# Two-layer image-prompt attention: even entries laid image first with one mixed value group, halves of the output added by VectorE out of PSUM, low parts of two splits on GpSimd

## The chip, the cores and the metric

One core of a Trainium2 chip runs the whole program in one launch. The metric is device time in microseconds (us), lower is better. Engines are named as the profile names them: PE multiplies matrices (PEld loads its weights), DVE is VectorE, ACT is ScalarE, POOL is GpSimd, SP issues most transfers.

## The reference

Two attention layers follow one another over 16 batch entries of 256 queries and 256 context rows (E = 512 wide), with 320 channels (C) in 20 heads (H) of 16 (D). The first layer, cut to what matters:

```python
q = heads(x @ Wq)
text, image = ctx[:, :77], ctx[:, 77:]              # 77 and 179 rows
a_text  = softmax(q @ heads(text @ Wk).T * scale)
a_image = softmax(q @ heads(image @ Wk_ip).T * scale + semantic_term)
out = a_text @ heads(text @ Wv) + mask * (a_image @ heads(image @ Wv_ip))
x = x + out.reshape(...) @ Wout + bout
```

The semantic term is built from a second, narrow softmax over the products of the text rows with the image rows (in the kernel `tokens0`, `semantic0`, `rs`). The second layer does the same kind of work with 252 text rows and 4 image rows; the change hardly touches it.

## The kernel before

The code's comments call the layers 0 and 1. A layer is cut into 80 slots: slot k treats entry `b = k // 5` and one group of four heads, `g = k % 5`. A layer-0 slot does, per half t of the context:

- `score0`: scores with queries on the partitions, S, from which DVE takes two maxima per head, of text and image (L747, L748); `maxima0` (L754) turns them for the stacked operands.
- `turned0`: transposed scores T, keys on the partitions (L770); ACT writes their exponentials into a P tile (L773), and POOL multiplies these by the semantic weights `rs` (L776).
- `attend0(k-1)`: 24 matmuls (L805) with values `vr` into the values' bank, also called P in the profile. `vr` holds three blocks of 128 context rows per entry: rows 0 to 127 as text (its mask zeroes the image rows), rows 0 to 127 as image, rows 128 to 255 as image. Text and image outputs lie in the two halves of the bank.
- `settle0`: DVE transposes the bank (L816), takes reciprocals of the sums (L819, L820) and multiplies (L822) into `tmp`; POOL adds the halves (L823) into `hsn`, and copies the last group (L825).

Around the slots run tasks with written due times in slots. For each pair c of entries `keys0(c)` loads the context of both, splits it into a high and a low part (tiles `cta`, `ctb`; high on ACT, low on POOL, L169) and makes the keys of both (128x156 text, 128x360 image). `tokens0` makes the text-image products, `values0_` the values: three groups per entry, each of 12 matmuls of 320 columns (`wC` holds the text weights and `wD` the image weights). `queries0` splits the input `xq` into `hq` (L284 on ACT, L285 on POOL, L286 on DVE). After an entry's last slot `gather` transposes `hsn` on DVE (L835), and `finish` splits the result into `ho` (L284 on ACT, L285 and L286 on DVE) and projects it (L611, L614). PE's order and the start (`begin`, all engines) are written by hand; inside a slot the other engines' instructions are ordered by a scheduler.

Of the kernel before, what the change touches and what calls it, by code (L numbers as in the profile page):

```python
# [35 lines left out]
CH = H * D  # L36

# [15 lines left out]
def xattn2(  # L53
# [60 lines left out]
    words, slots = {"ctb": 1024, "cta": 1024, "raw": 512, "rawc": 512, "both": 2 * (S - T0), "kb": 936, "si": 256, "sp": 128, "wC": 2 * 4 * (H * D + NIP), "mt": S, "mx": 2, "tmp": (NG + 1) * 48, "kst": 4 * S, "rs": 2 * S, "P": 4 * S}, {}  # L114
# [47 lines left out]
    def halves(hi, lo, src, eng=nc.vector, loaded=False):  # L162
        order = queued if loaded else lambda inst: inst
        if len(hi.shape) != len(src.shape):
            src = src.rearrange("p (d h) -> p d h", d=D)[:, :, :H]
        order(nc.scalar.copy(hi, src))
        for i, (to, *at) in enumerate(lo if isinstance(lo, list) else [(lo,)]):
            at = (slice(None), *at)
            order((nc.gpsimd if i and loaded else eng).tensor_sub(to, src[at], f(hi)[at]))  # L169
# [22 lines left out]
    def in_turn(parts, wait, tag="raw", eng=nc.vector, later=False):  # L192

        ahead, parts, tags = [], list(parts), tag.split()
        for i in range(len(parts) + 1):
# [4 lines left out]
            if i:  # L200
                halves(*ahead.pop(0), eng, wait)
# [52 lines left out]
    def evacuate(hi, lo, out, m):  # L254

        if m < 2:
            return halves(hi, lo, out)
        hi, lo = hi[:64], lo[:64]
        both = buf("both", list(hi.shape), bufs=2)
        nc.scalar.copy(hi, out[:64])  # L260
        nc.scalar.copy(both, out[64:])
        nc.vector.tensor_sub(out[:64], out[:64], f(hi))
        nc.vector.tensor_add(lo, out[:64], both)

    def context(b, n, wait=0):

        tiles, parts = [], []
        for k in range(0, 4, 3 - n):
            src = cT_d[:, b * S : (b + n) * S].rearrange("(k p) t -> p k t", p=128)[:, k : k + 3 - n]
            ct = buf("cta" if n == 1 or k < 2 else "ctb", [128, 2, 512], FR, bufs=SIZES["CTA" if n == 1 or k < 2 else "CTB"], name="ct")  # L270
            split = lambda t: t.rearrange("p (k t) -> p k t", t=n * S)
            parts.append((src, split(ct[:, 0]), split(ct[:, 1])))
            tiles.append(ct)
        yield from in_turn(parts, wait, "rawc raw" if b == 2 and n == 2 else "rawc", nc.gpsimd if wait and b != 2 else nc.vector, n == 2 and b > 2)
        if n == 2:
            return lambda s, k: tiles[k][:, s].rearrange("p (b t) -> p b t", b=2)
# [3 lines left out]
    def split(src, neg, eng, tag, place=None):  # L280
# [5 lines left out]
        order(nc.vector.scalar_tensor_tensor(hl[:, 2], f(hl[:, 2]), neg, src[:, 2], op0=ALU.mult, op1=ALU.add))  # L286
        return hl

    ct = [buf(t, [128, 2, 512], FR, bufs=2, name="ct") for t in ("cta", "cta", "ctb", "ctb")]
    ct0 = {0: lambda s, k, tiles=ct: tiles[k][:, s].rearrange("p (b t) -> p b t", b=2)}  # L290
# [10 lines left out]
    for k in range(4):  # L301
        first["c", k] = cT_d[k * 128 : (k + 1) * 128, : 2 * S], ct[k][:, 0], ct[k][:, 1], ("rawc", "raw")[k // 2]
# [8 lines left out]
    ks = [const_tile([128, 4, S], f"ks{i}", FR) for i in range(SIZES["NR"])]  # L311
# [54 lines left out]

    def keys0(c):
        if c not in ct0:
# [3 lines left out]
            get("m0t", 2 * c - 1)  # L372
            ct0[c] = yield from tiles
        ct = ct0[c]
        kt = kts[c] = buf("kb", [128, 3, 2, 2, T0 + 1], FR, name="kt")
        for m in range(3):
            kst = buf("kst", [128, 2, 2, S], FR, bufs=SIZES["KST"])
            for w, lo, hi, a, z in ((wk0, 0, T0 + 1, 0, T0), (wki0, T0 - 1, S, T0, S)):
                kp = bank()[:, : 2 * (hi - lo)].rearrange("p (b t) -> p b t", b=2)
                prod_m(kp, w, m, lambda s, k: ct(s, k)[:, :, lo:hi], 4)  # L380
                n = 64 if m == 2 else 128
                evacuate(kst[:, 0, :, a:z], kst[:, 1, :, a:z], kp[:, :, a - lo : z - lo], m)
                if a:
                    keys_out(kd[0][c], m, kst)
                else:
                    nc.gpsimd.tensor_copy(kt[:n, m, :, :, :T0], f(kst[:n, :, :, :T0]))
                yield

    def keys_first():

        ct = ct0[0]
        kst = [buf("kst", [128, 2, 2, S], FR, bufs=SIZES["KST"]) for i in range(2)]
        kst.append(buf("ho", [128, 5 * S], FR)[:, : 4 * S].rearrange("p (s b t) -> p s b t", s=2, b=2))
# [3 lines left out]
        kp = [out(0, T0 + 1) for m in range(3)]  # L397
        for k in range(4):
            for m in range(3):
                terms = ((0, 0), (0, 1), (1, 0))[: 3 if m < 2 else 2]  # L400
                for i, (a, c) in enumerate(terms):
                    mm(kp[m], wk0(a, k, m), ct(c, k)[:, :, : T0 + 1], start=k + i == 0, stop=k == 3 and i == len(terms) - 1)
            yield
        for m in range(3):
            n = 64 if m == 2 else 128
            evacuate(kst[m][:, 0, :, :T0], kst[m][:, 1, :, :T0], kp[m][:, :, :T0], m)
            nc.gpsimd.tensor_copy(kt[:n, m, :, :, :T0], f(kst[m][:n, :, :, :T0]))
        yield
        for m in range(3):
            kp = out(T0 - 1, S)  # L410
            prod_m(kp, wki0, m, lambda s, k: ct(s, k)[:, :, T0 - 1 : S], 4)
            evacuate(kst[m][:, 0, :, T0:], kst[m][:, 1, :, T0:], kp[:, :, 1:], m)
            keys_out(kd[0][0], m, kst[m], slice(0, 1))
            yield
        for m in range(3):
            keys_out(kd[0][0], m, kst[m], slice(1, 2))
        yield

    def values0_(b):
        ct, i = ct0[b // 2], b % 2  # L420
        V = vr[(b + 2) % 3]
        for t, (w,), lo, sc in ((0, wv0, 0, tmask[:, 0:1]), (1, wvi0, 0, tmask[:, 1:2]), (2, wvi0, 128, 1.0)):
            vp = bank()[:, :320]
            prod(vp, lambda s, k: ct(s, k)[:, i, lo : lo + 128], lambda s, k: w(s, k), 4)
# [3 lines left out]
            yield  # L428
        return V

    def tokens0(b):

        ct, i = ct0[b // 2], b % 2
        stack = buf("M", [TR, 2, S], FR, bufs=SIZES["M"])
        M = stack[:T0]
        nc.gpsimd.memset(f(M[:, :, :T0]), 0.0)
        gp = bank()
        lo = 64
        prod(gp[:T0, : S - lo], lambda s, k: ct(s, k)[:, i, :T0], lambda s, k: ct(s, k)[:, i, lo:S], 4)
        src = gp[:T0, T0 - lo : S - lo]  # L440
# [213 lines left out]
    def semantic0(b):  # L654
# [41 lines left out]
        for t in range(2):  # L696
            mm(rp[:, t], mh[:T0, 0, t * 128 : (t + 1) * 128], tph[:, 1], start=True, stop=False)
            mm(rp[:, t], mh[:T0, 1, t * 128 : (t + 1) * 128], tph[:, 0], start=False, stop=True)
# [7 lines left out]
    def stacks0(k, parts="KQTM"):  # L706
        b, g = divmod(k, NG)
        Q, K = QK[k] = qs[k % SIZES["NR"]], ks[k % SIZES["NR"]]
        for part in parts:
# [4 lines left out]
            elif g < SIZES["NR"]:  # L714
# [3 lines left out]
                else:  # L718
                    dma(K[XROW : XROW + TR, :, T0:], mh[:, 0:1, T0:].to_broadcast([TR, 4, S - T0]))
# [19 lines left out]
    def score0(k, t):  # L739
# [7 lines left out]
        nc.vector.tensor_reduce(mn[:, t, :, 0], sp[:, :, :T0], axis=AX.X, op=ALU.max)  # L747
# [721 lines left out]
```

## Time and profile before

| what | us |
|---|---|
| median of 3 runs (range) | 1493.27 (1488.1 to 1494.71) |
| profiled execution: time, span | 1491.16, 1489.3 |
| busy: PE, DVE, ACT, POOL | 1426.1, 1172.7, 886.0, 1212.5 |
| layer 0, ten slots (one pair of entries) in the steady part | 74.5 |

The chain of waits is 75% PE, 8% DVE, 5% DMA and 5% POOL. Layer 0 ends near 700 us of the span. Rows of instructions give start, duration, engine, line, operation and tile; a row of the stretches gives, after its length, each engine's busy time and count, then the clock granted to PE, the share of the DMA engines and GB/s. Neighbouring instructions of one engine overlap in the records, so a group of matmuls is timed best from its first start to the next group's.

### The profile page before, as it was taken

The numbers are of one execution on the slowest core, as the hardware profiler recorded it, in microseconds if no ns is written. First come the engines' busy times: TensorE is split into PE (matmuls) and PEld (weight loads), VectorE is DVE, ScalarE is ACT, GpSimd is POOL, SyncE is SP. The second block draws the span as 40 slices with busy tenths as digits, with TensorE's granted clock in tenths as the row PEclk, the third lists the DMA queues.
The fourth block names the chain that finished last, engine by engine and source line by source line (L and its number), as shares of the span: only waits on it lengthen the run. The fifth ranks groups of instructions, "written<-read, shape, count | busy, mean of one in ns | idle before, by whom it ended". The sixth has DMA issues, their size and how long they took to land.

```text
span 1489.3 us, 36118 instructions
## 1 busy us (share of the span) xinstructions
PE 1426.1 (96%) x12740; PEld 1155.8 (78%) x12740; DVE 1172.7 (79%) x2595; ACT 886.0 (59%) x1975; POOL 1212.5 (81%) x1302
## 2 busy tenths in 40 slices
PE   8799999999999899789999999999999999999998
PEld 7678888888888788577777777777777777777766
DVE  5467777777777787778887788788878887888787
ACT  5346565656565555456665666566666665666563
POOL 4359797979797877798698779878987898788887
PEclk9799999999999999799999999999999999999999
DMA  7867777778787776684534444444444444444411
GB/s 237 212 178 222 205 223 205 222 204 224 200 228 202 208 204 176 165 222 151 155 104 126 123 117 119 133 122 116 121 133 119 121 121 124 125 122 102 112 32 55
DMA packets 230986, 234.32 MB, mean 157 GB/s; under 512 B 39127, under 2 KB 200678, under 8 KB 230790
## 3 DMA queue, kind: packets, MB, share of 16 engines
q1 hardware_dynamic: 228598, 230.71, 55.8%
q8 instruction: 102, 1.67, 0.5%
q10 hardware_dynamic: 2208, 1.30, 0.4%
q14 instruction: 78, 0.64, 0.1%
HBM read 118.04 MB, written 77.04 MB: 131 GB/s over the span
## 4 chain that ended last, share of the span: by engine, by line
PE 75%; DVE 8%; DMA 5%; POOL 5%; issue 3%; ACT 3%; SPq 1%; ACTq 0%; DVEq 0%; POOLq 0%
PE X L944 15%; PE X L241 14%; PE P L805 6%; PE X L611 5%; PE S L746 5%; PE P L956 5%; PE P L966 4%; PE T L770 4%; PE T L895 3%; PE S L901 3%; PE X L614 2%; PE X L251 2%; PE X L580 2%; DVE mn L748 2%; POOL P L776 1%
## 5 line engine op out<-in xcount | busy, mean ns | idle before, releaser
L776 POOL TENSOR_TENSOR P<-P,rs 128x512 f32<-128x512 f32 x320 | 414.4, 1318 | 86.6 <-ACT P L773 79.8
L935 POOL TENSOR_TENSOR wt<-P,ctb 128x512 f32<-128x512 f32 x318 | 408.4, 1308 | 74.1 <-ACT ctb L933 74.0
L944 PE MATMUL X<-ctb,gm 128*128 128x512 f32 x1120 | 306.3, 402 | 5.8 <-DVE wt L945 5.7
L773 ACT ACTIVATE P<-T 128x512 f32<-128x512 f32 x320 | 175.4, 594 | 159.4 <-PE T L770 112.4
L945 DVE TENSOR_TENSOR wt<-X,wt 128x512 f32<-128x512 f32 x320 | 216.1, 681 | 42.2 <-PE X L944 37.3
L944 PEld LDWEIGHTS X<-ctb,gm 128*128 128x128 f32 x1120 | 195.0, 188 | 39.3 <-DVE wt L945 8.7
L915 ACT ACTIVATE P<-T 128x512 f32<-128x512 f32 x320 | 173.1, 593 | 75.1 <-PE T L895 72.1
L933 ACT ACTIVATE ctb<-P 128x512 fp32r<-128x512 f32 x320 | 186.6, 627 | 38.0 <-PE X L944 35.2
L903 DVE TENSOR_REDUCE mn<-S 128x4 fp32r<-128x1008 f32 x160 | 191.5, 1197 | 0.0
L748 DVE TENSOR_REDUCE mn<-S 128x4 fp32r<-128x716 f32 x160 | 142.4, 890 | 0.0
L805 PE MATMUL P<-P,vr 128*32 128x256 f32 x1920 | 125.9, 393 | 6.1 <-DVE tmp L822 2.2
L746 PE MATMUL S<-ks,qs 125*128 125x256 f32 x640 | 117.4, 307 | 6.2 <-DMA ks<-M 4.1
L746 PEld LDWEIGHTS S<-ks,qs 125*128 125x128 f32 x640 | 89.0, 195 | 40.8 <-issue 22.1
L1035 POOL TENSOR_TENSOR r<-u,rs 128x40 f32<-128x40 f32 (+2 forms) x17 | 108.7, 6395 | 3.1 <-DVE u L1032 3.0
L770 PE MATMUL T<-qs,ks 127*128 127x256 f32 x640 | 107.7, 291 | 0.4 <-DMA qs<-mt 0.3
L747 DVE TENSOR_REDUCE mn<-S 128x4 fp32r<-128x308 f32 x160 | 74.5, 466 | 31.1 <-PE S L746 31.0
L816 DVE STREAM_TRANSPOSE nt<-P 128x512 f32<-128x512 f32 x80 | 57.1, 713 | 52.9 <-PE P L805 52.2
L805 PEld LDWEIGHTS P<-P,vr 128*32 128x32 f32 x1920 | 56.7, 112 | 47.4 <-POOL P L776 7.3
L770 PEld LDWEIGHTS T<-qs,ks 127*128 127x128 f32 x640 | 91.6, 197 | 1.7 <-DMA qs<-mt 0.8
L956 PE MATMUL P<-P,v1t 128*32 128x256 f32 x1280 | 85.7, 385 | 0.0
L966 PE MATMUL P<-wt,zone 128*32 128x256 f32 x1280 | 84.4, 379 | 0.0
L241 PE MATMUL X<-wC,cta 128*128 128x324 f32 (+1 forms) x474 | 78.4, 312 | 0.0
(305 smaller groups left out, 2976.8 us busy)
## 6 DMA issues: line engine op xcount, KB each, us to landing
qd<-q SPq DMA_DIRECT2D x96, 256.0 KB
qs<-tph SPq DMA_DIRECT2D x64, 320.0 KB
rawc<-in_cT_dram SPq DMA_DIRECT2D x60, 256.0 KB
qs<-qd SPq DMA_DIRECT2D x80, 192.0 KB
ks<-kd SPq DMA_DIRECT2D x80, 192.0 KB
ks<-kd SPq DMA_DIRECT2D x160, 96.0 KB
qs<-qd SPq DMA_DIRECT2D x160, 96.0 KB
kd<-kst SPq DMA_DIRECT2D x57, 256.0 KB
```

What stands on the lines that cost most here:

```text
L241: last = mm(out, lhs(a, k), rhs(b, k), start=i == 0, stop=i == len(terms) - 1)
L746: mm(sp[:, h], Q[: XROW + T0, h, t * 128 : (t + 1) * 128], K[: XROW + T0, h], start=True, stop=True)
L770: mm(st[p][:, j], K[:KS0, 2 * p + j, t * 128 : (t + 1) * 128], Q[:KS0, 2 * p + j], start=True, stop=True)
L773: exp = anchor(nc.scalar.activation(pt, st[p], AF.Exp, scale=SCALE))
L776: anchor(nc.gpsimd.tensor_mul(pt, pt, rs[:, t : t + 1].to_broadcast([128, 2, S])))
L805: mm(pv[32 * s : 32 * s + 32, o : o + S], v[:, vt, h : h + 32], P[k, s // 2][:, t, s % 2], start=vt < 2, stop=vt != 1,)
L903: anchor(nc.vector.tensor_reduce(maxes[k + 2][:, t], sp[:, :, :T1], axis=AX.X, op=ALU.max))
L915: anchor(nc.scalar.activation(P[k, u][:, t], st[u], AF.Exp, scale=SCALE))
L933: nc.scalar.activation(R[k, u][:, t], P[k, u][:, t], AF.Copy, scale=0.5)
L935: anchor(eng.tensor_sub(W[k, u][:, t], P[k, u][:, t], f(R[k, u][:, t])))
L944: mm(yp, gm[:, gb], R[k, u][:, kt], start=i == 0, stop=i == len(blocks[n]) - 1)
L945: nc.vector.tensor_mul(W[k, u][:, n], yp, W[k, u][:, n])
```

## The change

Even entries are laid with their 179 image rows first and the 77 text rows behind, odd entries text first as before. One group of 12 matmuls, `values_mixed`, then makes the image values that lie beside text in both entries of a pair (51 rows of the even one, 51 of the odd one), so a pair has five value groups instead of six. The context tiles become padded tiles of 1129 words with 51 words of zeros ahead and sides of 539 words; their splits are written in two pieces, text and image, and so are the image keys' evacuations. The masks in the sum column of `vr` now differ by entry and are set by `mark(b)` for each entry, in place of one `marks()`; the memsets of `M` in `tokens0` go to the start. `settle0` multiplies into the values' bank instead of `tmp`, and a DVE reduction over a stride of 128 words adds the halves into `hsn`. `split_pool` makes the low parts of layer 0's `ho` on POOL; `queries0` makes the last low part of `hq` on POOL too. In layer 1 the copy of the last group goes into DVE's multiplication.

PE, ahead of slot 10c+5: 24 value matmuls stood behind the transposed scores of the slot before (`ident_r` rows are L754, the next slot's maxima).

```order
350 L746 MATMUL S<-ks_99,qs_95 128x256 x4
351 L770 MATMUL T<-qs_97,ks_101 128x256 x4
352 L241 MATMUL X<-wD,cta_81 128x320 x3
353 L241 MATMUL X<-wD,cta_82 128x320 x3
354 L241 MATMUL X<-wD,ctb_83 128x320 x3
355 L241 MATMUL X<-wD,ctb_84 128x320 x3
356 L241 MATMUL X<-wD,cta_81 128x320 x3
357 L241 MATMUL X<-wD,cta_82 128x320 x3
358 L241 MATMUL X<-wD,ctb_83 128x320 x3
359 L241 MATMUL X<-wD,ctb_84 128x320 x3
360 L754 MATMUL X<-ident_r,mn_566 8x128 x2
```

The same place after:

```order
342 L840 MATMUL S<-ks_99,qs_95 128x256 x4
343 L865 MATMUL T<-qs_97,ks_101 128x256 x4
344 L252 MATMUL X<-wD,cta_81 128x320 x3
345 L252 MATMUL X<-wD,cta_82 128x320 x3
346 L252 MATMUL X<-wD,ctb_83 128x320 x3
347 L252 MATMUL X<-wD,ctb_84 128x320 x3
348 L849 MATMUL X<-ident_r,mn_614 8x128 x2
```

One group of 12 is gone there; elsewhere in the steady part PE's order is the same, with 180 columns for 192 and 154 for 156 in some groups.

POOL, in slots 10c+5 and 10c+6 of a pair, before (P rows are L776; `rawc` is the loaded context):

```order
205 L776 TENSOR_TENSOR P_120<-P_120,rs_115 128x512
206 L776 TENSOR_TENSOR P_121<-P_121,rs_115 128x512
207 L169 TENSOR_TENSOR cta_81<-rawc_118,cta_81 128x512
208 L823 TENSOR_TENSOR hsn<-tmp_808 128x8x16
209 L169 TENSOR_TENSOR cta_82<-rawc_117,cta_82 128x512
210 L776 TENSOR_TENSOR P_122<-P_122,rs_115 128x512
211 L776 TENSOR_TENSOR P_123<-P_123,rs_115 128x512
```

And after:

```order
226 L327 TENSOR_TENSOR hq_270<-xq_91,hq_270 128x512
227 L329 TENSOR_TENSOR hq_270<-xq_91,hq_270 64x256
228 L871 TENSOR_TENSOR P_121<-P_121,rs_116 128x512
229 L871 TENSOR_TENSOR P_122<-P_122,rs_116 128x512
230 L934 TENSOR_TENSOR ho_195<-hT_1335,ho_195 128x256
231 L871 TENSOR_TENSOR P_121<-P_121,rs_116 128x512
232 L871 TENSOR_TENSOR P_122<-P_122,rs_116 128x512
233 L175 TENSOR_TENSOR cta_81<-rawc_119,cta_81 128x154
234 L175 TENSOR_TENSOR cta_81<-rawc_119,cta_81 128x2x179
235 L175 TENSOR_TENSOR cta_82<-rawc_118,cta_82 128x154
236 L175 TENSOR_TENSOR cta_82<-rawc_118,cta_82 128x2x179
237 L871 TENSOR_TENSOR P_123<-P_123,rs_116 128x512
```

The additions into `hsn` are gone from POOL, and splits of `hq` and `ho` stand between the products.

DVE, where an entry's last group is settled and its output split, before:

```order
508 L816 STREAM_TRANSPOSE nt_136<-P 128x512
509 L835 STREAM_TRANSPOSE hT_1300<-hsn 128x256
510 L747 TENSOR_REDUCE mn_567<-S 128x4
511 L748 TENSOR_REDUCE mn_567<-S 128x4
512 L819 RECIPROCAL P<-nt_136 128x16
513 L285 TENSOR_TENSOR ho_161<-hT_1300,ho_161 128x512
514 L286 SCALAR_TENSOR_TENSOR ho_161<-ho_161,tmask,hT_1300 128x256
515 L820 TENSOR_TENSOR P<-P,mk 128x8
```

And after:

```order
524 L914 RECIPROCAL P<-nt_136 128x16
525 L915 TENSOR_TENSOR P<-P,mk 128x8
526 L917 TENSOR_TENSOR P<-nt_136,P 128x256
527 L923 TENSOR_REDUCE hsn<-P 128x8x16 x2
528 L277 TENSOR_TENSOR kst_193<-X,kst_193 128x179 x2
529 L944 STREAM_TRANSPOSE hT_1335<-hsn 128x256
```

The two `ho` rows are gone from DVE; one or two reductions stand behind each multiplication.

The diff, cut to its core:

```diff
+MIX = S - T0 - 128
+CI = 2 * T0
+CG = 128 + T0
+CW = CI + CG + S - T0 + 1
...
+    def padded(tag):
+        return buf(tag, [128, MIX + 2 * CW], FR, bufs=2, name="ct")
+    def side(t, s, at, n):
+        at += MIX + s * CW
+        return t[:, at : at + n]
+    def texts_of(t, s):
+        return side(t, s, 0, CI).rearrange("p (b t) -> p b t", b=2)
+    def images_of(t, s, more=0):
+        return side(t, s, CW - 2 * CG, 2 * CG).rearrange("p (b t) -> p b t", b=2)[:, :, CG - S + T0 - 1 : CG - 1 + more]
...
+        for of in cut:
+            nc.vector.tensor_sub(of(out if m == 2 else lo), of(out), f(of(hi)))
...
-    order(nc.vector.scalar_tensor_tensor(hl[:, 2], f(hl[:, 2]), neg, src[:, 2], op0=ALU.mult, op1=ALU.add))
+        if neg is None:
+            order(eng.tensor_sub(hl[64:, 2], src[64:, 2], f(hl[64:, 2])))
...
-            nc.gpsimd.memset(f(ks[i]), 0.0)
+            nc.gpsimd.memset(f(ksw[i]), 0.0)
...
+        for t in ct:
+            nc.gpsimd.memset(f(t[:, :MIX]), 0.0)
+            for s in range(2):
+                nc.gpsimd.memset(f(side(t, s, CI + S - T0, CG - S + T0)), 0.0)
+                nc.gpsimd.memset(f(side(t, s, CW - 1, 1)), 0.0)
...
+    def mark(b):
+        V = vr[(b + 2) % 3]
+        for t, m in enumerate(masks(b)):
+            nc.gpsimd.tensor_copy(vcols(V, V0W)[:, t, :, 16], m.to_broadcast([128, H]))
+        return V
...
             dma(ks[i][XROW + T0 : KS0, :, :T0], ind0r[:2, :T0].unsqueeze(1).to_broadcast([2, 4, T0]))
+            dma(ksw[i][XROW + T0 : KS0, 4 * S :], ind0r[:2, :T0])
...
+    def value_rows(ct, at, w, *to):
+        vp = bank()[:, :320]
+        prod(vp, lambda s, k: side(ct[k], s, at, 128), lambda s, k: w(s, k), 4)
+        for V, t, sc in to:
...
+    def values_mixed(c):
+        to = [(vr[(b + 2) % 3], 1, masks(b)[1]) for b in (2 * c, 2 * c + 1)]
+        value_rows(ct0[c], CI + 128, wvi0[0], *to)
...
-        nc.gpsimd.memset(f(M[:, :, :T0]), 0.0)
...
-        tmp = buf("tmp", [128, 2, 8, 16], bufs=2)
-        nc.vector.tensor_mul(tmp, nt[:, :, :, 0:16], rz.unsqueeze(3).to_broadcast([128, 2, 8, 16]))
-        nc.gpsimd.tensor_add(hn[:, g // 2, :, g % 2], tmp[:, 0], tmp[:, 1])
+        tmp = pv[:, 16:272]
+        nc.vector.tensor_mul(
+            tmp.rearrange("p (a f d) -> p a f d", a=2, f=8), nt[:, :, :, 0:16], rz.unsqueeze(3).to_broadcast([128, 2, 8, 16])
+        )
+        tmp = tmp.rearrange("p (a f d) -> p f d a", a=2, f=8)
         if g == NG - 1:
-            nc.gpsimd.tensor_copy(hn[:, 2, :, 1], hn[:, 2, :, 0])
+            for i in range(2):
+                nc.vector.tensor_reduce(hn[:, 2, :, i], tmp, axis=AX.X, op=ALU.add)
             later(0.45, lambda: gather(0, b))
+        else:
+            nc.vector.tensor_reduce(hn[:, g // 2, :, g % 2], tmp, axis=AX.X, op=ALU.add)
+
+    def split_pool(src, neg, tag):
+        hl = buf(tag, [128, 5, S], FR)
+        nc.scalar.copy(hl[:, 0:2], src[:, 0:2])
+        nc.scalar.activation(hl[:, 2], src[:, 2], AF.Copy, scale=neg)
+        nc.gpsimd.tensor_sub(hl[:, 3:5], src[:, 0:2], f(hl[:, 0:2]))
+        nc.gpsimd.tensor_add(hl[:, 2], src[:, 2], f(hl[:, 2]))
+        return hl
...
-        task(("v0", 2 * c), shifted(n, -7, -5.4, -5), lambda b=2 * c: values0_(b), *k)
-        task(("v0", 2 * c + 1), shifted(n, -4, -3.8, -3.4), lambda b=2 * c + 1: values0_(b), *k)
+        task(("v0", 2 * c), shifted(n, -7, -5.4), lambda b=2 * c: values0_(b), *k)
+        task(("vm", c), shifted(n, -4.2), lambda c=c: values_mixed(c), *k)
+        task(("v0", 2 * c + 1), shifted(n, -3.8, -3.4), lambda b=2 * c + 1: values0_(b), ("vm", c))
```

More of the change, by code (lines that the diff above doesn't have):

```diff
@@ L200, in in_turn @@
             if i:
-                halves(*ahead.pop(0), eng, wait)
+                hi, lo, src = ahead.pop(0)
+                if isinstance(hi, list):
+                    for piece in zip(hi, lo, by_side(src)):
+                        halves(*piece, eng, "pieces")
+                else:
+                    halves(hi, lo, src, eng, wait)
             for j in new:
@@ L396, in keys_first @@
         out = lambda lo, hi: bank()[:, : 2 * (hi - lo)].rearrange("p (b t) -> p b t", b=2)
-        kp = [out(0, T0 + 1) for m in range(3)]
+        kp = [out(0, T0) for m in range(3)]
         for k in range(4):
@@ L649, in queries0 @@
         yield
-        xs = split(x, tmask[:, 5:6], nc.gpsimd, "hq") if b else xs0.pop()
+        xs = split(x, None, nc.gpsimd, "hq") if b else xs0.pop()
         yield
```

189 lines of the change are left out of this document (117 added, 72 removed).

## The prediction

> **What bounds the kernel now.** I read the busy times first, then stretches of the span, then what PE waits for in them.
>
> ```profile
> PE 1426.1 (96%) x12740; PEld 1155.8 (78%) x12740; DVE 1172.7 (79%) x2595; ACT 886.0 (59%) x1975; POOL 1212.5 (81%) x1302
> 349.00:423.50 74.50, 73.45 (x701) 63.62 (x701) 57.95 (x137) 44.12 (x104) 65.70 (x64) 1.00 0.78 214
> 339.70:377.50 37.80, 37.57 (x358) 32.56 (x354) 29.67 (x71) 22.54 (x55) 36.02 (x37) 1.00 0.80 228
> 377.50:414.20 36.70, 35.88 (x347) 31.05 (x350) 28.29 (x66) 21.60 (x51) 29.71 (x28) 1.00 0.76 201
> 500.00:600.00 100.00, 89.74 (x809) 76.15 (x807) 80.09 (x182) 53.42 (x130) 77.69 (x88) 0.97 0.72 196
> 600.00:735.00 135.00, 122.04 (x1075) 94.92 (x1076) 107.52 (x230) 78.83 (x176) 107.06 (x125) 0.92 0.62 173
> ```
>
> Behind each stretch stand its length and the busy time of PE, PEld, DVE, ACT and POOL. One pair of entries takes 74.50 us, and PE is busy in 73.45 of them: the steady part of layer 0 is PE's. But POOL's load is uneven. In slots 5 to 9 of a pair (339.7 to 377.5) it is busy 36.02 of 37.80 us, in the other five 29.71 of 36.70. From 500 to 735 us, where layer 0 runs out, PE is idle for 10.3 and 13.0 us. What PE waits for, first from 200 to 480, then from 485 to 735 (total, times, longest):
>
> ```profile
> PE X L611 <- ACT mt L756: 3.2, 4, 0.8
> PE X L754 <- DVE mn L748: 7.2, 11, 2.3
> PE P L805 <- DVE tmp L822: 2.2, 2, 1.8
> PE P L805 <- POOL P L776: 1.5, 2, 0.9
> ```
>
> In 280 us of the steady part the longest sum is 3.2 us, and POOL is not named; at the end of the layer it is DVE, by its maxima (L748), that ends most waits.
>
> **The value group.**
>
> ```profile
> 402.58 1.04 PE L241 MATMUL X<-wD,cta 128*128 128x320 f32 x6
> 403.46 1.04 PE L241 MATMUL X<-wD,ctb 128*128 128x320 f32 x6
> 404.34 0.28 PE L754 MATMUL X<-ident_r,mn 128*8 128x128 f32 x2
> ```
>
> Twelve matmuls take 404.34 − 402.58 = 1.76 us, with nothing else on PE beside them. One such group leaves each pair. Columns 192 to 180 and 156 to 154 I cost at nothing: these groups are short, and their bound is −0.1 us a pair. Layer 0 has eight pairs. Pair 0's group falls in the start, where PE waits for transfers, and I count nothing for it. Pair 7's, near 565 us, lies where layer 0 ends and DVE shares the bound: I count 1.0 of 1.76. Six are wholly PE's: 6 × 1.76 = 10.6.
>
> **POOL.** What it loses and gets per pair, from these rows (mean ns):
>
> ```profile
> L776 POOL TENSOR_TENSOR P<-P,rs 128x512 f32<-128x512 f32 x161 | 207.7, 1314 | 27.9 <-ACT P L773 27.3
> L823 POOL TENSOR_TENSOR hsn<-tmp 128x128 f32<-128x128 f32 x40 | 20.2, 506 | 2.2 <-DVE tmp L822 2.2
> L169 POOL TENSOR_TENSOR cta<-rawc,cta 128x512 fp32r<-128x512 f32 x8 | 11.0, 1377 | 0.0
> L169 POOL TENSOR_TENSOR ctb<-rawc,ctb 128x512 fp32r<-128x512 f32 x8 | 10.3, 1290 | 0.0
> L386 POOL CAST kb<-kst 128x308 fp32r<-128x308 f32 x8 | 3.5, 437 | 0.0
> L825 POOL COPY hsn<-hsn 128x128 f32<-128x128 f32 x8 | 2.3, 288 | 0.0
> L436 POOL MEMSET M<- 77x154 f32 x8 | 1.8, 227 | 2.1 <-PE X L698 2.0
> ```
>
> Between 128 and 512 elements a two-input operation grows by (1290 − 506) / 384 = 2.0 ns an element, so estimates are 0.74 us for 256 elements, 0.55 for 154 and 0.98 for 358. Away go ten L823 (5.1), two L825 (0.6), two L436 (0.5), four context splits (5.3) and three casts (1.3): 12.8. In come two splits of `ho` at 1.29 + 0.74 (4.1), two last parts of `hq` (1.5), four context splits in two pieces at 0.55 + 0.98 (6.1), six casts of half the size (some 0.3 each, 1.8) and four mask copies (near L436, 0.25 each, 1.0): 14.5. So POOL gets about +1.7 us per pair: 67.4 of 73 us, still below PE on average. One thing gives back:
>
> ```profile
> 346.51 0.92 POOL L823 TENSOR_TENSOR hsn<-tmp 128x128 f32<-128x128 f32 x1
> 355.04 0.46 POOL L823 TENSOR_TENSOR hsn<-tmp 128x128 f32<-128x128 f32 x1
> 345.45 1.66 DVE L285 TENSOR_TENSOR ho<-hT,ho 128x512 fp32r<-128x512 f32 x1 [1.36 <-ACT ho L284]
> ```
>
> The same addition takes 0.92 beside DVE's split of `ho` and 0.46 alone. With `ho` and `hq` gone from DVE such overlaps go, about 0.5 to 1 us per pair. The Trainium skill has this rule ("SBUF — State Buffer", Who interferes with whom): a DVE instruction with two SBUF inputs contends with a GpSimd instruction that reads SBUF, one with a single SBUF input doesn't. The two rows agree, and by the rule the reductions, which read PSUM, cost POOL nothing.
>
> But the place matters. The saved PE time lies in the light half (402 us), the new POOL work in the heavy one: there go five L823 (2.8 as they ran), L825, L436, the four old splits (5.3) and three casts, 9.9 in all, and there come two `ho` splits' parts (3 of 4.1), a first `hq` that now falls behind the marks (1.3 moved, and two last parts 1.5), the new context splits (6.1), casts and marks (2.4): 14.3. 36.0 + 4.4 less 1 of contention is 39.4 us of POOL in 37.8 of PE. So POOL falls up to 1.6 us behind and makes it up in the other half, which has 7 us to spare. The four P tiles are two slots' worth, and POOL enters slot 5 ahead by about a half-slot; following its new order against PE's attends I find about 1.6 us of slack left in slots 6 to 8 and 0.1 to 0.3 in slot 9 and the next 0. The stall lies between 0 and 1.6 us per pair; I take 0.4, near the walk. ACT, at 22.5 of 37.8 us, hides its added casts.
>
> **DVE.**
>
> ```profile
> L748 DVE TENSOR_REDUCE mn<-S 128x4 fp32r<-128x716 f32 x80 | 71.2, 890 | 0.0
> L747 DVE TENSOR_REDUCE mn<-S 128x4 fp32r<-128x308 f32 x80 | 37.3, 466 | 7.6 <-PE S L746 7.5
> L285 DVE TENSOR_TENSOR ho<-hT,ho 128x512 fp32r<-128x512 f32 x8 | 9.3, 1164 | 5.4 <-ACT ho L284 5.4
> L286 DVE SCALAR_TENSOR_TENSOR ho<-ho,tmask,hT 128x256 fp32r<-128x256 f32 x8 | 8.8, 1103 | 0.0
> L286 DVE SCALAR_TENSOR_TENSOR hq<-hq,tmask,xq 128x256 fp32r<-128x256 f32 x8 | 4.8, 603 | 0.9 <-ACT hq L284 0.8
> ```
>
> Away per pair: 2 × (1.16 + 1.10 + 0.60) = 5.7. The reductions are new. By L747 and L748, (890 − 466) / 408 = 1.04 ns an element and 0.15 fixed, 256 elements take 0.41 us; if reading every 128th word halves the rate, 0.68. Twelve per pair: 4.9 to 8.2. I take 0.5, near the row. Key evacuations in two pieces add three fixed parts, 0.45. Sum −0.4 to +2.9 on 57.95 of 74.5: DVE stays under 85%. The values' bank is held one reduction longer, 0.4 to 0.7 us, twice that in slot 4; in the steady part nothing waits for it (no L805 in the waits up to 480), so nothing is charged. Near the end of the layer L805 waited 2.2 us for L822, and there it counts.
>
> **The end of the layer, 485 to 735.** On the chain stand, among much else:
>
> ```profile
> 537.59 1.52 DVE ho L286
> 622.39 0.77 DVE ho L285
> 623.75 1.50 DVE ho L286
> 668.99 1.44 DVE ho L286
> 681.48 1.29 POOL P L776
> ```
>
> There are seven such pieces of `ho`, three of about 1.5 and four of 0.5 to 0.8, some 7 us; they leave DVE; on POOL the same split costs 2.0, and POOL is itself on the chain near 681. Reductions and their longer hold of the bank take back about 4. I take −1, bounds −5 and +4.
>
> **The start.**
>
> ```profile
> 4.03 0.62 ACT L1265 CAST cta<-rawc 128x512 fp32r<-128x512 f32 x1 [2.02 <-DMA rawc<-in_cT_dram]
> 5.84 0.88 POOL L395 MEMSET kb<- 128x936 f32 x1
> 17.61 3.54 SPq L86 DMA_DIRECT2D ks<-mt  x4
> 8.21 2.03 PE L402 MATMUL X<-cta,wA 128*128 128x156 f32 x8 [0.87 <-ACT wA L1265]
> 32.67 2.36 DMA kd<-ho
> ```
>
> ACT's first image cast ran at 4.03; its tile is now first zeroed in part on POOL, which was free of its other memsets at 5.84. PE's first keys, from 8.21, come 0.3 to 1.4 us later. SP issues four more transfers like the four that took 3.54, 2.7 to 3.5 us of its queue, ahead of `kd<-ho` on the chain; part of it is waited away. Together 0 to +3.5, taken +1.5. Layer 1 loses 16 POOL copies of 0.29 that lie beside PE work: nothing.
>
> **Sum.** 6 × (1.76 − 0.4) = −8.2; pair 7 −1.0; end −1; start +1.5: −8.7. The profiled execution, 1491.16 us (span 1489.3), would become 1482.5; it lies 2.1 below the median of 1493.27, so the forecast is about 1484.5, −0.6%. What a measurement can tell from no change is 0.5%, 7.5 us: faster means under 1485.8, slower over 1500.7.
>
> **Rivals.**
>
> *POOL takes the gain.* If slots 5 to 9 overrun by the whole 1.6 us, or the 2.0 ns slope is too low for pieces of 154 and 179, each pair gives 1.6 back: 6 × 0.16 + 1 + 1 − 1.5 leaves −1.5, 1492; range 1488 to 1496. For it: 36.02 of 37.80. Against: four P tiles, and 7 us idle in the other half.
>
> *The full gain.* No stall, and the end of the layer gives 5: −10.6 − 1.8 − 5 + 1 = −16, 1477; 1473 to 1480.
>
> *PE reads the padded context slower (the other side).* The rows of `cta` and `ctb` now begin at odd words in about half the cases (word offsets 51 and 205 of the high side, against 128 and 410). As the streamed operand they feed keys and tokens:
>
> ```profile
> 361.19 1.14 PE L241 MATMUL X<-cta,wB 128*128 128x360 f32 x6
> 362.18 1.16 PE L241 MATMUL X<-ctb,wB 128*128 128x360 f32 x6
> ```
>
> Six of 360 columns take 0.99 us, 0.46 ns a column. Per pair 32 × 360 + 32 × 154 + 24 × 180 = 20,800 columns, half of them odd: 4.8 us. A third slower there (+1.6) eats the gain less the stall; twice as slow gives +4.8 per pair: 7 × (4.8 − 1.36) + 1 = +25, 1518. It decides for slower from about 1.5 times (+2.3 per pair). No row of the trace streams from an odd word. The Trainium skill's page "Vector Engine (DVE) Microarchitecture Reference", The SBUF access granule: adjacent pairs, gives 1.30 ns against 1.05 for pairs that begin on an odd word, on VectorE; were it to hold for PE, an estimate by that page is +1.15 us per pair, 7 × (1.15 − 1.36) + 0.5 = −1, about 1492.
>
> *The start or the end of the layer worsens.* With `ho` behind POOL's products and the bank held longer, the end could take +4 and the start +3.5 with stalls of 0.8: −5.8 − 1 + 7.5 = +1, 1494; up to 1500.
>
> **Chances.** The forecast (1479 to 1489) 0.47; POOL takes the gain 0.18, of which 0.02 above 1500.7 should pieces cost far more than estimated; the full gain 0.11; slower streaming 0.12, of which 0.08 above; a worse start or end 0.12, of which 0.05 above. Faster is the full gain and 0.7 of the forecast, 0.44; slower 0.15; same 0.41. The range, 1474 to 1500, leaves out the slow streaming and the edges.
>
> **What would show it.** Per pair 73.1 us instead of 74.5, and 12 fewer `wD` matmuls ahead of slot 10c+5. Waits of L805 for POOL's P in slots 8 to 10 of a pair: up to 0.4 us a pair bears me out, 1.5 the rival. Groups of 360 columns at 0.99 us per six: more, and the odd words cost. The reduction between 0.41 and 0.68 us, 256-element POOL pieces at 0.74, L823-like doubling gone. PE's first matmul (8.21 before) at 8.5 to 9.6. The prediction is wrong if DVE's mean row for the reduction is above 0.8 us, if POOL is idle under 2 us per pair, or if PE waits more than before between 485 and 735.

## The result, and the profile after

The changed kernel takes 1506.6 us (median of 6 runs, 1503.2 to 1508.3) where the kernel before takes 1492.83: 1.009 of it, 95% interval 1.0066 to 1.0114. It is slower by 13.8 us, outside the range, and on the other side of the forecast: over the 1500.7 that the prediction set for slower. The profiled execution took 1506.93 us, its span 1505.2.

The page's busy times, then stretches of the trace. The first three stretches are one pair of entries each (from one mixed value group to the next).

```profile
PE 1415.6 (94%) x12644; PEld 1144.9 (76%) x12644; DVE 1179.0 (78%) x2676; ACT 891.9 (59%) x2047; POOL 1208.9 (80%) x1324
259.16:335.26 76.10, 71.92 (x691) 62.06 (x689) 58.84 (x146) 45.18 (x113) 65.74 (x66) 1.00 0.78 210
335.26:411.36 76.10, 71.22 (x683) 61.09 (x681) 58.01 (x144) 44.60 (x112) 65.08 (x66) 1.00 0.78 209
411.36:487.46 76.10, 72.39 (x689) 62.23 (x690) 58.91 (x146) 45.39 (x114) 65.97 (x67) 1.00 0.80 210
500.00:600.00 100.00, 90.19 (x803) 77.28 (x803) 71.67 (x173) 53.74 (x136) 78.53 (x92) 0.93 0.72 188
600.00:735.00 135.00, 116.40 (x1085) 90.66 (x1084) 110.20 (x247) 76.41 (x174) 105.63 (x111) 0.97 0.69 181
```

PE's work per pair fell from 73.45 to about 71.9 us, a fall near the 1.76 forecast. Its idle time rose from 1.0 to 4.2, so a pair takes 76.1 us instead of 74.5. POOL is no busier than before (65.1 to 66.0 us), DVE hardly (58.0 to 58.9 after 57.95). What PE waits for, from 200 to 480 (seven rows), then from 500 to 690 (the two longest sums):

```profile
PE X L252 <- DVE sp L764: 4.3, 4, 1.1
PE X L707 <- ACT mt L851: 3.5, 4, 1.5
PE P L900 <- DVE mx L767: 2.4, 3, 0.8
PE X L704 <- ACT mt L851: 2.1, 4, 0.5
PE P L900 <- DVE hsn L926: 1.8, 4, 0.4
PE S L840 <- DMA qs<-mt: 0.9, 1, 0.9
PE T L865 <- DMA qs<-mt: 0.9, 3, 0.3
PE X L849 <- DVE mn L843: 9.9, 9, 2.4
PE P L900 <- DVE hsn L926: 4.3, 4, 2.1
```

POOL is again not named in the steady part. L900 is the attend (L805 before), L926 the reduction. The row with `mx` is the reduction's too: by the instructions around it PE was waiting for the values' bank. First DVE's rows there, then PE's:

```profile
330.47 0.42 DVE L917 TENSOR_TENSOR P<-nt,P 128x256 f32<-128x256 f32 x1
330.80 0.23 DVE L764 TENSOR_TENSOR sp<-sp,X 128x77 f32<-128x77 f32 x1
330.94 0.15 DVE L768 TENSOR_SCALAR mx<-mx 128x1 f32<-128x1 f32 x1
331.00 0.47 DVE L842 TENSOR_REDUCE mn<-S 128x4 fp32r<-128x308 f32 x1
331.39 0.89 DVE L843 TENSOR_REDUCE mn<-S 128x4 fp32r<-128x716 f32 x1
332.20 0.41 DVE L926 TENSOR_REDUCE hsn<-P 128x128 f32<-128x256 f32 x1
332.76 1.50 PE L900 MATMUL P<-P,vr 128*32 128x256 f32 x24 [0.80 <-DVE mx L767]
```

The product (L917) ends at 330.89, the reduction at 332.61, and the next attend starts at 332.76. The reduction takes 0.41 us, but four other instructions stand between it and its product, so the bank stays taken 1.7 us longer. In the kernel before, the same four stood behind the product (L822), and nothing that the bank needed stood behind them:

```profile
322.40 0.41 DVE L822 TENSOR_TENSOR tmp<-nt,P 128x256 f32<-128x256 f32 x1
322.73 0.23 DVE L671 TENSOR_TENSOR sp<-sp,X 128x77 f32<-128x77 f32 x1
322.87 0.15 DVE L675 TENSOR_SCALAR mx<-mx 128x1 f32<-128x1 f32 x1
322.94 0.47 DVE L747 TENSOR_REDUCE mn<-S 128x4 fp32r<-128x308 f32 x1
323.32 0.89 DVE L748 TENSOR_REDUCE mn<-S 128x4 fp32r<-128x716 f32 x1
```

Over 41 settlings between 190 and 500 us the reduction starts 0.34 us after its product in the mean and 1.31 at most; it ends, and gives the bank back, 0.83 us after it in the mean. What matters is each slot's slack in the kernel before, from the end of its product to the start of the next attend. In slot 3 of a pair the bank is now held 1.72 us beyond the product, where the slack was 0.72 to 1.02; in slot 9 it is held 1.13, where the slack was 0.78 to 0.92. In slot 1 the slack was only 0.15, but there the changed kernel has its product earlier, 3.0 us ahead of the attend. In the other seven slots the slack, 2.7 us or more, is longer than the hold.

The start of each attend, taken from PE's rows, shows where the time went; the difference to the kernel before, in us:

| kernel | first attend | slot 4 | slot 14 | slot 54 | slot 79 | us per pair, slots 14 to 54 |
|---|---|---|---|---|---|---|
| after | +3.2 | +3.5 | +4.2 | +11.2 | +13.8 | 76.40 (before 74.65) |

So the start loses 3.2 us, each pair some 1.75, the end of layer 0 another 2.6, and layer 1 the remaining 2.1 of the span, which I did not look into. Within a pair the gain is there: attend 24 lags 1.83 us less than attend 23. The other slots lose 3.4: slots 3 and 9 of a pair wait for the bank, slot 8 for `sp`, slot 7 for ACT's `mt`, and slot 5 in part for the transfers `qs<-mt`.

### The profile page after: what moved, and what is told of

It reads as the page before. It is cut to its first block, busy times and chain, and to the rows that moved or that the text cites. A ratio compares the mean times of both kernels' runs of the same rounds, so it can differ in the third digit from the quotient of the medians.

```text
span 1505.2 us, 36245 instructions
## 1 busy us (share of the span) xinstructions
PE 1415.6 (94%) x12644; PEld 1144.9 (76%) x12644; DVE 1179.0 (78%) x2676; ACT 891.9 (59%) x2047; POOL 1208.9 (80%) x1324
## 4 chain that ended last, share of the span: by engine, by line
PE 67%; DVE 10%; DMA 8%; POOL 6%; issue 4%; ACT 3%; SPq 1%; ACTq 1%; POOLq 0%; DVEq 0%
PE X L1053 14%; PE X L252 12%; PE P L900 6%; PE X L704 5%; PE P L1065 4%; PE S L840 4%; PE P L1075 4%; PE T L1004 3%; PE S L1010 3%; PE T L865 3%; DMA qs<-mt 2%; PE X L262 2%; PE X L707 2%; POOL wt L1044 2%; DVE mn L843 2%
## 5 line engine op out<-in xcount | busy, mean ns | idle before, releaser
L871 POOL TENSOR_TENSOR P<-P,rs 128x512 f32<-128x512 f32 x320 | 407.2, 1293 | 118.9 <-ACT P L868 117.4
L1024 ACT ACTIVATE P<-T 128x512 f32<-128x512 f32 x320 | 173.1, 594 | 73.4 <-PE T L1004 70.9
L900 PE MATMUL P<-P,vr 128*32 128x256 f32 x1920 | 126.1, 392 | 16.0 <-DVE hsn L926 7.7
L900 PEld LDWEIGHTS P<-P,vr 128*32 128x32 f32 x1920 | 57.8, 112 | 57.3 <-POOL P L871 15.8
L272 ACT CAST kst<-X 128x179 fp32r<-128x179 f32 (+5 forms) x117 | 36.2, 329 | 83.0 <-PE X L252 44.7
```

The costliest lines, as they stand in the source:

```text
L871: anchor(nc.gpsimd.tensor_mul(pt, pt, rs[:, t : t + 1].to_broadcast([128, 2, S])))
L900: mm(pv[32 * s : 32 * s + 32, o : o + S], v[:, vt, h : h + 32], P[k, s // 2][:, t, s % 2], start=bool(start), stop=bool(stop),)
L1024: anchor(nc.scalar.activation(P[k, u][:, t], st[u], AF.Exp, scale=SCALE))
```

## The experiments

Each kernel ran with 3 rounds, best_ho and best_mix with 5, in groups on three chips. The table has the median, the ratio to the kernel before (same chip, 95% interval), and from the profiled execution the same slots as above.

| kernel | us | ratio | slot 4 | us per pair | slot 79 |
|---|---|---|---|---|---|
| after | 1506.6 | 1.009 [1.0066, 1.0114] | +3.5 | 76.40 | +13.8 |
| a_sbuf | 1490.27 | 0.9986 [0.9962, 1.0009] | +1.0 | 74.58 | +2.0 |
| a_add | 1536.46 | 1.0291 [1.025, 1.0332] | −0.9 | 80.65 | +39.6 |
| a_ho | 1501.49 | 1.005 [1.0021, 1.0079] | +4.4 | 74.99 | +6.1 |
| a_layout | 1506.39 | 1.0068 [1.0034, 1.0102] | +0.9 | 77.40 | +9.3 |
| b_bank | 1520.07 | 1.0193 [1.0131, 1.0255] | +3.0 | 78.91 | +27.7 |
| b_sbuf | 1512.35 | 1.0126 [1.0087, 1.0164] | −1.5 | 78.30 | +16.9 |
| a_sbuf_ho | 1491.67 | 0.999 [0.9962, 1.0019] | +0.2 | 73.77 | +0.4 |
| a_sbuf_hq | 1491.55 | 0.998 [0.9956, 1.0005] | +0.0 | 75.19 | −0.7 |
| a_sbuf_start | 1487.98 | 0.9965 [0.9937, 0.9993] | −4.1 | 74.51 | −6.2 |
| best_ho | 1488.76 | 0.9972 [0.9951, 0.9993] | −3.8 | 73.91 | −6.5 |
| best_mix | 1484.96 | 0.995 [0.993, 0.9971] | +1.0 | 73.78 | −0.5 |
| a_tight | 1532.82 | 1.0251 [1.0209, 1.0293] | +2.0 | 78.13 | +41.9 |

A difference of two kernels in us is one of raw medians, and their chips can differ; the kernel before had medians of 1492.4 to 1496.3 beside these runs. The ratio allows for the chip.

The profiled start varies: best_ho and best_mix have the same start, and slot 4 lies 4.8 us apart in their executions. So the start is judged by medians below, and the pairs by the traces. The clock granted to PE varies too, late in layer 0 above all. In slots 54 to 64 the same 723 matmuls kept PE busy for 77.9 us in best_ho (granted clock 0.98), 81.8 in the changed kernel (0.93) and 84.7 in a_sbuf (0.89). So a few us between two traces there can be the clock alone; what sets it, these runs don't show.

**a_sbuf**: the product into an SBUF tile; DVE's work stays, the bank is free after the product.

```diff
-        tmp = pv[:, 16:272]
+        tmp = buf("tmp", [128, 256], bufs=2)
```

> The changed kernel, but the product goes to an SBUF tile and DVE reduces from there: DVE's work stays, the values' bank is free one reduction earlier. If the hold of the bank is what costs, the attends' waits of 0.4 and 0.8 us a pair go: 74.9 us a pair, about 1499. If DVE's time and order cost, 76 us a pair, 1505. A reduction that reads SBUF at a stride may also be slower than the 0.42 us measured.

The time falls by 16.3 us (15.5 by the ratios), to that of the kernel before or a little below; a pair takes 1.8 us less. The reduction takes 0.42 us from SBUF too, and at slot 33 DVE's order is that of the changed kernel, with the same four instructions ahead of it; but the attend no longer waits for it:

```profile
324.92 1.50 PE L900 MATMUL P<-P,vr 128*32 128x256 f32 x24
325.23 0.42 DVE L926 TENSOR_REDUCE hsn<-tmp 128x128 f32<-128x256 f32 x1
```

So what differs is the hold. The waits from 200 to 480 have no row of the attend any more:

```profile
PE X L252 <- DVE sp L764: 4.6, 4, 1.4
PE X L707 <- ACT mt L851: 4.4, 4, 1.8
PE X L704 <- ACT mt L851: 2.1, 4, 0.5
PE S L840 <- DMA qs<-qd: 0.2, 1, 0.2
```

The hold of the bank is shown as the largest cause, and larger than expected: the attends' own waits were about 1.1 us a pair, and those for `qs<-mt`, 0.5 a pair, went with them.

**a_add**: the settling as before, everything else changed.

```diff
+        tmp = buf("tmp", [128, 2, 8, 16], bufs=2)
...
+        nc.gpsimd.tensor_add(hn[:, g // 2, :, g % 2], tmp[:, 0], tmp[:, 1])
```

> The changed kernel with the settling as before: product into tmp, POOL adds and copies, no DVE reduction, values' bank free after the product. Theory R (the reduction costs: it holds the values' bank and stands in DVE's queue): a pair of entries goes from 76.1 to 74 us or less, the waits of the attends for DVE (0.4 and 0.8 us a pair) and of the key group for sp (1.1) go, time about 1492 to 1495. Theory L (the layout in two pieces costs): 75.5 to 76 us a pair, 1503 or more. Theory O (the low parts of ho on POOL cost): as L.

Missed: it is slower than any of the three theories had it. With the additions back POOL has marks, `ho`, `hq` and them: 70.0 us busy in a pair of 80.6, and PE waits for it by name:

```profile
PE X L704 <- POOL ho L929: 8.6, 3, 2.9
PE X L707 <- DVE xc L955: 7.1, 4, 2.5
```

L929 is POOL's low part of `ho`. The reduction on DVE is what makes room on POOL for the splits; the two cannot be separated by undoing the one. The size isn't clean, though: the granted clock was 0.96 to 0.98 in these pairs, and PE's own work 73.6 to 75.4 us where it was 71.9 at 1.00.

**a_ho**: `ho` split by DVE again.

```diff
-        hh = split(hT, tmask[:, 6:7], nc.vector, "ho") if l else split_pool(hT, tmask[:, 6:7], "ho")
+        hh = split(hT, tmask[:, 6:7], nc.vector, "ho")
```

> The changed kernel with layer 0's ho split by DVE as before (L285 and L286 of before). Theory O: the waits of the output projections (0.9 us a pair and more) go, 75 us a pair, about 1498. Theory R: DVE gets 2.3 us more per entry, the waits for DVE grow: 76.5 or more, 1508 and above. Theory L: no change.

1.4 us a pair and 5 us in all come back, though DVE gets more work. Theory O holds as a second cause. Theory R's longer waits don't come: those for DVE fall from 8.5 to 6.9 us between 200 and 480, though 2.8 of them are new, for the maxima and `q`.

**a_layout**: settling, `ho` and `hq` all undone; the layout, its pieces, marks and start stay.

```diff
-        xs = split(x, None, nc.gpsimd, "hq") if b else xs0.pop()
+        xs = split(x, tmask[:, 5:6], nc.gpsimd, "hq") if b else xs0.pop()
...
-        hh = split(hT, tmask[:, 6:7], nc.vector, "ho") if l else split_pool(hT, tmask[:, 6:7], "ho")
+        hh = split(hT, tmask[:, 6:7], nc.vector, "ho")
...
+        nc.gpsimd.tensor_add(hn[:, g // 2, :, g % 2], tmp[:, 0], tmp[:, 1])
```

> The changed kernel with settling, ho and hq all as before; what stays is the layout with one mixed value group, its pieces, the marks and the start. If R and O hold together: 73 us a pair (74.5 less 1.76 and some 0.3 of pieces), about 1486. Theory L: 75 or more, 1500. The start stays late by about 3 us in every case.

77.4 us a pair, as theory L had it: the layout alone loses 2.75 us a pair where its one group fewer should give 1.76. Here PE waits 5.0 us in 280 for ACT's `ho` cast and 1.8 for DVE's `ho`. A part of the 2.75 seems to go with the granted clock: in four of the pairs between slots 4 and 54 it was 0.98, with 73.4 to 74.2 us of PE work; the fifth ran at 1.00, with 72.1, and took 75.1 us. Its runs spread widely too, from 1493.99 to 1513.09. So the parts don't seem to add, and the layout seems to need some of the other moves; that is argued, not shown.

**b_bank** and **b_sbuf**: the kernel before with the reduction alone, from the bank and from SBUF.

```diff
-        tmp = buf("tmp", [128, 2, 8, 16], bufs=2)
+        tmp = pv[:, 16:272]
...
-        nc.gpsimd.tensor_add(hn[:, g // 2, :, g % 2], tmp[:, 0], tmp[:, 1])
+            nc.vector.tensor_reduce(hn[:, g // 2, :, g % 2], tmp, axis=AX.X, op=ALU.add)
```

b_sbuf has `tmp = buf("tmp", [128, 256], bufs=2)` in the first place.

> The kernel before with one part of the change alone: settle0 multiplies into the values' bank and DVE reduces from there (POOL's additions and copies in layer 0 gone). If the longer hold of the bank is the cause by itself, attends wait 1.2 us or more per pair for DVE and a pair goes from 74.5 to 75.7 to 76.3: 1503 to 1507. If it only costs together with the new layout or the fuller POOL, 74.5 and no difference from before.

> The kernel before with the reduction on DVE, reading an SBUF tile, in place of POOL's additions: DVE's work as in the run with the bank (4.5 us a pair slower than before), the bank free after the product as before. If the hold of the bank costs there as in the changed kernel (1.7 us a pair), 77.3 us a pair, about 1508. If nearly all of the 4.5 us are the hold, 74.5 to 75 and 1493 to 1497. If nearly all are DVE's load (5 us more per pair on 58), 78 to 79 and 1514 to 1520.

From the bank a pair takes 4.3 us more than before, beyond both outcomes expected; from SBUF 3.65. The hold is 0.6 us a pair there (in all 7.7 us by the medians, 10 by the ratios, on two chips); the rest comes with DVE's added work, 65.8 busy of 78.1 us. Of the 7.9 us added, the twelve reductions are 5.1; the other 2.8 are DVE's splits of `ho` and `hq`, as many as before but longer (between 190 and 500 us L285 takes 2.33 in the mean against 1.22, the last part of `hq` 0.96 against 0.60). In b_sbuf PE waits most for DVE's key and query work:

```profile
PE X L251 <- DVE q L169: 5.2, 4, 1.3
PE X L241 <- DVE sp L671: 3.6, 4, 1.1
PE X L668 <- DVE q L263: 2.3, 4, 0.8
```

That DVE's load as such sets this is not shown: a_sbuf_ho, below, has 61.7 us of DVE in 73.9 (84%, the same share) and loses nothing. The order of its queue differs. For the longest of these waits the rows show how:

```profile
311.89 2.52 POOL L776 TENSOR_TENSOR P<-P,rs 128x512 f32<-128x512 f32 x2
311.92 3.05 DVE L285 TENSOR_TENSOR ho<-hT,ho 128x512 fp32r<-128x512 f32 x1
315.29 0.41 DVE L169 TENSOR_TENSOR q<-X,q 128x256 fp32r<-128x256 f32 x1
315.75 0.91 PE L251 MATMUL X<-cta,wB 128*128 128x360 f32 x4 [1.29 <-DVE q L169]
```

DVE's split starts just behind two POOL products, ends 0.56 us after them, and makes `q` and then PE late; so do the splits at 233.75, 389.24 and 466.96. In the kernel before the same split began ahead of the products:

```profile
306.88 0.67 DVE L285 TENSOR_TENSOR ho<-hT,ho 128x512 fp32r<-128x512 f32 x1
307.07 3.05 POOL L776 TENSOR_TENSOR P<-P,rs 128x512 f32<-128x512 f32 x2 [1.01 <-ACT P L773]
```

Where the other waits of b_sbuf come from stays open.

**a_sbuf_ho** and **a_sbuf_hq**: a_sbuf with `ho`, or the last part of `hq`, on DVE again, by the `ho` line of a_ho and the `xs` line of a_layout.

> The changed kernel with the product in SBUF and the reduction from there (1490 us, 74.3 us a pair), and ho's low parts back on DVE. The waits of the output projection for ACT's mt (1.1 us a pair) stand behind ACT's wait for the context load; if POOL's ho work makes that load late, they go: 73.2 us a pair, 1483. If they come from ACT's own order they stay, and DVE's 2.3 us more per entry lengthen the waits for sp: 74.5 to 75, 1492 to 1496.

> As the run with the product in SBUF, and the last low part of hq back on DVE. The wait of the image key group for DVE's sp (1.15 us a pair, 0.2 in one pair of before) comes from DVE's order: sp stands behind the maxima there, ahead of them before. If the missing hq operation shifted that order, it goes: 73.2 us a pair, about 1483. If not, 74.3 and 1490, or worse by DVE's 0.6 us per entry.

With `ho` on DVE a pair falls to 73.77, the wait for `sp` is gone and that of L707 for `mt` falls from 4.4 to 1.7. By slot 54 it leads the kernel before by 4.8 us, but the time stays where it was, at 1491.67 in place of 1483: attend 76 gives 6.4 us back. There stand, on POOL and on DVE:

```profile
656.03 5.00 POOL L871 TENSOR_TENSOR P<-P,rs 128x512 f32<-128x512 f32 x4
657.30 4.34 DVE L327 TENSOR_TENSOR ho<-hT,ho 128x512 fp32r<-128x512 f32 x1
```

DVE's split stood until POOL's run of four products was over, and the maxima behind it, for which PE waited 3.7 us. With `hq` on DVE nothing is gained: the wait for `sp` grows to 7.5 us; that theory fell.

**a_sbuf_start**: DVE zeroes the context tiles, and four early transfers into `ks` in place of eight; four small ones follow later.

```diff
-            nc.gpsimd.memset(f(t[:, :MIX]), 0.0)
+            nc.vector.memset(f(t[:, :MIX]), 0.0)
...
-            dma(ks[i][XROW + T0 : KS0, :, :T0], ind0r[:2, :T0].unsqueeze(1).to_broadcast([2, 4, T0]))
-            dma(ksw[i][XROW + T0 : KS0, 4 * S :], ind0r[:2, :T0])
+            dma(turned_ks[i][XROW + T0 : KS0, :, S - T0 :], ind0r[:2, :T0].unsqueeze(1).to_broadcast([2, 4, T0]))
...
+            dma(ksw[i][XROW + T0 : KS0, :T0], late[:2])
```

> As the run with the product in SBUF, with another start: the context tiles are zeroed by DVE instead of POOL, and of the eight early transfers into ks only four stay (the blocks that even entries use); four small ones follow after the first slots' loads. If the start's loss (first attend 3.3 us late, slot 4 1.0 late) is these two, the first attend comes 2 to 3.3 us earlier and the time is 1487 to 1489. If PE's first groups or the transfers for slot 0 set it anyway, under 0.5 us.

As expected, the median falls by 2.3 us, and the first attend comes 3.05 us earlier in the profile; but the runs of the two kernels overlap (1484.68 to 1493.78 and 1487.49 to 1496.74), and the 2.3 is not clear of their scatter. SP's rows, of after and of this kernel:

```profile
17.21 6.67 SPq L90 DMA_DIRECT2D ks<-mt  x8
17.35 3.67 SPq L90 DMA_DIRECT2D ks<-mt  x4
```

**best_ho** (a_sbuf_start with `ho` on DVE) and **best_mix** (the same, with the last two entries' `ho` on POOL, by the line below).

```diff
-        hh = split(hT, tmask[:, 6:7], nc.vector, "ho") if l else split_pool(hT, tmask[:, 6:7], "ho")
+        hh = split(hT, tmask[:, 6:7], nc.vector, "ho") if l or b < 14 else split_pool(hT, tmask[:, 6:7], "ho")
```

> Product in SBUF, ho's low parts on DVE, and the other start, together. If the gains add (start 5 us by slot 4, 1.0 us a pair), slot 54 stands 10 us ahead of before; the end of the layer took 5 back where ho was on DVE: 1481 to 1484, ratio 0.992.

> As the run before it, but the last two entries split ho on POOL. There DVE's split stood 4.3 us beside four products on POOL, and the maxima behind it; if that is what takes the 5 to 6 us back after slot 75, they stay: 1477 to 1480, ratio 0.989. If something else comes late there, as the run before it.

best_ho leads by 12.8 us at slot 69 and gives half of it back: no better than a_sbuf_start, and slower than the 1481 to 1484 expected. But not as a_sbuf_ho did: 5.0 of the 6.3 us are lost between slots 69 and 75, ahead of attend 76, and the split at that place stood only 1.79 us:

```profile
654.65 1.79 DVE L327 TENSOR_TENSOR ho<-hT,ho 128x512 fp32r<-128x512 f32 x1
```

best_mix is 3.8 us faster than best_ho by the medians, though their runs overlap (1480.79 to 1490.94 and 1483.78 to 1497.26), and beats both kernels, 0.995 [0.993, 0.9971]; less than expected. Its profiled execution was one of its slowest (1490.91), and it too gives 6.5 us back between slots 69 and 79, with `ho` on POOL. So the split caught behind POOL's products explains a_sbuf_ho's loss at attend 76; that it takes the gain in general is not shown. In slots 64 to 74 the granted clock was 0.90 in best_ho and 0.88 in best_mix, with 70.7 and 71.7 us of PE work, against 0.94 and 68.7 in a_sbuf_ho.

**a_tight**: changed kernel, the reduction forced ahead of the second half's maxima.

```diff
+        if t and k > 2:
+            queued(first, *summed)
```

> The changed kernel with one ordering added: the text maxima of a slot's second score half may not run on DVE before the reduction of the attend ahead of them. The reduction then stands right behind its product in the values' bank (0.03 us after it, 0.34 in the mean and up to 1.3 in the changed kernel). If the place of the reduction in DVE's queue is what holds the bank too long, the attends' waits (0.4 and 0.8 us a pair) go and the time falls towards the run with the product in SBUF: 1492 to 1498. If the 0.42 us of the reduction itself are, it stays at 1505. If the maxima, now later, hold the scores' only buffer, PE waits for mn instead and it gets slower: 1510 or more.

The attends' waits are gone, and it is 26 us slower: the maxima come late, and PE waits for them 25 times between 200 and 480.

```profile
PE X L851 <- DVE mn L845: 15.0, 25, 1.1
```

L851 is the turning of the maxima. So the third outcome came, and more strongly: of the two places that the reduction was given in DVE's queue, one makes the attends late and the other the maxima.

## Why the prediction was wrong, point by point

**The step that failed** is on DVE: "in the steady part nothing waits for it (no L805 in the waits up to 480), so nothing is charged". I set the longer hold at the reduction's own 0.4 to 0.7 us and looked for waits that were there already. The hold is set by the reduction's place in DVE's queue, up to 1.7 us, and in slots 3 and 9 the slack between product and next attend was smaller than that: at slot 33 of before the product ended at 322.81 and the attend began at 323.82. Its price is 16.3 us here (after against a_sbuf), 9.8 with `ho` on DVE (a_ho against a_sbuf_ho), 7.7 on the kernel before (b_bank against b_sbuf), by raw medians. None of the rivals had it: the last one names the bank, but for the end of the layer only. Without it the change is 0.9986 of the kernel before.

**The value group** was right: PE's work fell by about 1.6 us a pair, and the lag by 1.83 at the place named. But the step from PE's work to the time failed with the waits above: even without the hold, in a_sbuf, a pair takes 74.58 us, the 74.65 of before.

**POOL.** The forecast's stall of 0.4 us a pair came true nowhere in the steady part as a wait for P, and the rival that POOL takes the gain fell in that form. Durations came as estimated:

```profile
L871 POOL TENSOR_TENSOR P<-P,rs 128x512 f32<-128x512 f32 x157 | 198.5, 1285 | 36.8 <-ACT P L868 35.9
L175 POOL TENSOR_TENSOR cta<-rawc,cta 128x358 fp32r<-128x358 f32 x8 | 7.1, 884 | 0.0
L934 POOL TENSOR_TENSOR ho<-hT,ho 128x256 fp32r<-128x256 f32 x7 | 5.1, 734 | 0.3
L329 POOL TENSOR_TENSOR hq<-xq,hq 64x256 fp32r<-64x256 f32 x7 | 5.1, 733 | 0.6
L926 DVE TENSOR_REDUCE hsn<-P 128x128 f32<-128x256 f32 x31 | 13.0, 419 | 0.7
```

734 and 733 ns against 0.74; 884 against 0.98; the products fell from 1314 to 1285 with DVE's two-input work gone, and are at 1306 in a_ho, where `ho` is DVE's again. But `ho` on POOL cost 1.4 us a pair (after against a_ho) or 0.8 (a_sbuf against a_sbuf_ho). With it on DVE the waits for `sp` go and those for `mt` shrink; ACT's `mt` cast stands behind context casts that wait for their transfers. That POOL's later splits free the load buffers late and so delay those transfers fits this, but is only argued.

**DVE's reduction** took 0.42 us at a stride of 128 words: the lower end. The slower rate that I kept open for reading every 128th word did not appear.

**The padded context at odd words** costs nothing; that rival is refuted.

```profile
305.90 1.17 PE L252 MATMUL X<-cta,wB 128*128 128x360 f32 x6
306.90 1.17 PE L252 MATMUL X<-ctb,wB 128*128 128x360 f32 x6
307.91 0.57 PE L262 MATMUL X<-cta,wA 128*128 128x154 f32 x4
```

Six take 1.00 us against 0.99. The estimate of +1.15 us a pair that I made from the Trainium skill's "Vector Engine (DVE) Microarchitecture Reference", The SBUF access granule: adjacent pairs, isn't borne out for PE: these rows show no such price.

**The start** was sized at +1.5 and is +3.2 at the first attend in the profile. It does not come of this one execution: in all eight kernels with the changed start the first attend comes 2.5 to 3.3 us after that of before, in b_bank and b_sbuf, with the old one, 1.0 and 1.8 us ahead of it. With the two changes that the prediction named it comes at +0.27 (a_sbuf_start) and +0.34 (best_ho), but at +3.31 in best_mix. The medians regain 2.3 and 2.9, within their scatter. So SP's 3.0 us of transfers are a likely cause, more of it than I took; they were not tried apart from POOL's memsets.

**The end of the layer** was taken at −1 and lost 2.6. One of the prediction's signs of being wrong came with it: PE is busy for 219.8 of the 250 us from 485 to 735, 226.7 before. The rows name L926 with 4.3 us, but the attends waited as long for DVE before, 2.2 us for L822 and these:

```profile
PE P L805 <- DVE mx L675: 2.2, 1, 2.2
```

And a_sbuf, without the hold, loses 2.2 us there too. So the hold is not shown as the cause of this part, which is no larger than what the clock can do; it stays open.

With the three terms mended (bank, `ho`, start) best_mix lands at 1484.96. That this is near the forecast's 1484.5 is chance: a pair takes 73.8 us there, not the 73.1 forecast, and other terms differ too.

## What to carry to other kernels

When the last reader of a buffer moves to another instruction, the price is not that instruction's duration but its place in its engine's queue: count what stands ahead of it, and compare the new release with the next use, even where no wait shows. Read the margin (release to next use) in each slot of a period, not the list of waits. A bundle of moves can be worth something together though the parts tried alone lose (here the reduction, b_sbuf, and the layout, a_layout), so each is judged in the company in which it stays.

## What the runs showed of the hardware that I had not expected

A DVE subtraction with both inputs in SBUF, 128x512, stood 4.34 us beside four POOL products issued one behind the other (5.00 us), where the same form takes about 1.1 us in the mean of that run and 0.67 at its shortest: it ended 0.61 us after the last of them. In b_sbuf it stood 3.05 us behind two products; in best_ho, 1.79 us, it got in within a run of four. The Trainium skill, "SBUF — State Buffer", Who interferes with whom, says that such an instruction contends with a GpSimd instruction that reads SBUF; here the wait outlasted several of them. For an instruction with one SBUF input the same section excepts the perf modes with two ports; the prediction left that out. A reduction from PSUM at a stride of 128 words ran at 0.42 us for 256 elements, as fast as the slope of contiguous ones predicts.
